# Two reorderings in a fused transposed-attention and binary-convolution kernel: where the first term of a depthwise convolution is issued, and in what pieces the last units are stored

## The chip, the cores and the metric

The kernel runs on one core of one Trainium2 chip. The metric is the device time of one execution in microseconds (us), as the median of several executions. The profile is one further execution, taken by the hardware profiler; its span (from the first to the last instruction) is about 2 us shorter than the device time. Engines are named as the profile names them: PE is the matrix engine and PEld its weight loads, DVE the vector engine, ACT the scalar engine, POOL the GpSimd engine, SP the engine that here only issues transfers. `ACTq` and `SPq` are the instruction queues of ACT and SP, from which transfers are issued. A label such as L382 is a line of the kernel.

## The reference, cut to what matters

The input is one image of 384 channels and 192 x 192 pixels. Layer 0 normalises it by groups, makes q, k and v by a 1x1 convolution, takes the maximum over 2x2 pixels, applies a 3x3 depthwise convolution, lets the channels of a head attend to each other, and projects. Layer 1 is a 1x1 convolution with binary weights on signs of shifted channels. Both add their input.

```python
qkv = jnp.einsum('bchw,oc->bohw', x, w_qkv) + b_qkv[None, :, None, None]
qkv = qkv.reshape(b, 3 * c, hs, DS, ws, DS).max(axis=(3, 5))
qkv = lax.conv_general_dilated(qkv, w_dw, (1, 1), 'SAME', feature_group_count=3 * c, ...)
qkv = qkv + b_dw[None, :, None, None]
q, k, v = jnp.split(qkv, 3, axis=1)
# ... cut: q and k normalised, attn = q k^T over pixels, four top-k softmaxes
out = _topk_softmax(attn, C // 2) @ v * a1 + ...      # three more of the same form
out = jax.nn.gelu(out, approximate=False)
out = repeat each pixel 2 x 2; out = jnp.einsum('bchw,oc->bohw', out, w_proj) + b_proj
# layer 0: x = x + L0(group_norm(x))
# layer 1: x = x + einsum(shifted sign(group_norm(x)), sign(weight)) + bias
```

## The kernel before

The image is cut into 24 units of 8 rows (4 rows after the maximum). The kernel makes four passes: sums for the normalisation; q and k (with the products q k^T); v with the attention applied to it; and a last pass with projection, residual, binary convolution and the store. Within a pass each unit has three tiles of 128 channels, m = 0, 1, 2.

In the v pass the result of the convolution goes to a `chunk`, which holds the rows of four units (UC = 4, CR = 16 rows of 96 columns). The convolution of unit u makes the rows 4u - 1 to 4u + 2, because its last row needs the next unit. So for u = 4, 8, 12, 16 and 20 one of the four rows belongs to the chunk before and three to the next: such a tile crosses a chunk, and `parts` has two entries, of 96 and of 288 elements per partition, instead of one of 384.

```python
# v pass
lo, hi = rows(u)
first = PR * u - 2 + lo
last = first + hi - lo
for m in range(CT):
    parts = []
    for c in range(first // CR, last // CR + 1):
        r0, r1 = max(first, c * CR), min(last, c * CR + CR - 1)
        parts.append(
            (chunk[c][:, m, (r0 - c * CR) * WP : (r1 + 1 - c * CR) * WP], r0 - first, r1 + 1 - r0)
        )
    if qkv_unit(pqkv, xt, u, 2 * CT + m, pool[m], parts, amid=lambda: block and next(block, 1)):
        block = None
    # ... cut
```

One tile is made in `qkv_unit`. Three blocks of 512 pixels are multiplied on PE (nine products, 18 instructions in the trace), each into one of three PSUM buffers; DVE takes the maximum out of each (L364) and so frees it. ACT adds the bias to the four new rows (L373). Then comes the convolution, nine terms on each part: the first on ACT (L380), eight on DVE (L382), each of which needs the one before. The first row of a part needs `pl` rows 0, 1 and 2; rows 0 and 1 are the last two of the unit before, copied there by ACT (L385), and only row 2 is new. `amid` lets a block of the attention be issued (`ops` in the trace: 32 matrix instructions into four PSUM buffers, emptied by ACT with GELU, L671).

```python
for r0, nr, c0, ncol in BLOCKS:
    ps = pqkv.tile([P, 512], F32, name="qkv")          # three buffers
    for t in range(CT):
        ins = nc.tensor.matmul(ps, wq[:, t, m * P : (m + 1) * P], x4[...], ...)   # L354
        # ... cut
    nc.vector.tensor_reduce(pl[...], ps.rearrange(...), AX.XY, ALU.max)           # L364
# ... cut
new = pl[:, 2 : 2 + PR, 1 : 1 + WP]
nc.scalar.activation(new, new, AF.Identity, bias=bq[:, m : m + 1])                # L373
for acc, r0, n in parts:
    acc2 = acc.rearrange("p (r w) -> p r w", w=WP)
    for k in range(9):
        r = lo - 1 + r0 + k // 3
        src = pl[:, r : r + n, k % 3 : k % 3 + WP]
        if k == 0:
            nc.scalar.activation(acc2, src, AF.Identity, bias=..., scale=...)     # L380
        else:
            nc.vector.scalar_tensor_tensor(acc2, src, wdw[:, m, k : k + 1], acc2, ALU.mult, ALU.add)  # L382
result = amid()
if u < NU - 1:
    nc.scalar.copy(pl[:, 0:2, :], pl[:, PR : PR + 2, :])                          # L385
```

In this pass the order of each engine's instructions is not that of the program: the compiler sets it beforehand, from the dependences and from its own estimate of when each instruction can start. On the chip the order is then fixed. `tc.keep_in_program_order(ins)` pins `ins` behind the instruction that the program has just before it on the same engine.

The last pass is issued in the order of the program. Its units go through `finished(i, m)`: two groups of four rows, each with six matrix products (L844) and one DVE addition (L856) into `xt`. The last three units, i = 21, 22, 23, are stored from there.

```python
def finished(i, m):
    u = order[i]
    xt, sg = kept[u], signs[i % NSIGN]
    for r0 in range(0, UR, 4):
        # ... cut: matmuls of four rows into ps (L844)
        last = (i, m) == (NU - 1, CT - 1)
        for js in (range(1), range(1, 2)) if last else (range(2),):
            px = slice((r0 + 2 * js[0]) * W, (r0 + 2 * js[-1] + 2) * W)
            blk = xt[:, m, px].rearrange("p (j n) -> p j n", j=len(js))
            nc.vector.scalar_tensor_tensor(blk, ps[...], bl1[:, m : m + 1], blk, ALU.add, ALU.add)   # L856
            if last:
                (nc.scalar if js[0] else nc.sync).dma_start(ov[u, :, m, px], xt[:, m, px])           # L860
    if i + 3 >= NU and (i, m) != (NU - 1, CT - 1):
        nc.sync.dma_start(ov[u, :, m], xt[:, m])                                                     # L862
```

Of the kernel before, what the change touches and what calls it, by code (L numbers as in the profile page):

```python
# [15 lines left out]
AF = mybir.ActivationFunctionType  # L16
# [6 lines left out]
CT = C // P  # L23
# [9 lines left out]
NU = H // UR  # L33
# [116 lines left out]
def conv_preact_kernel(ctx: ExitStack, tc: tile.TileContext, a: dict, out: bass.AP):  # L150
    nc = tc.nc
    xv = a["x"].rearrange("u t p n -> u p t n")
    ov = out.rearrange("u t p n -> u p t n")
# [10 lines left out]
    parts = {name: small[:, i:j] for name, i, j in SMALL}  # L164
    ind = parts["ind"].rearrange("p (t g) -> p t g", t=CT)
    bpr, bl1, bq, bdw, temp = (parts[i] for i in ("b_proj", "bias", "b_qkv", "b_dw", "temp"))
    wdw = parts["w_dw"].rearrange("p (m k) -> p m k", m=NM)
# [11 lines left out]
    def unit(u, pool=big, parts=1, pieces=1):  # L179
        xt = pool.tile([P, CT, UPX], F32, name="xt", tag="big")  # L180
        n = CT // parts
        for t in range(0, CT, n):

            for j in range(0, UPX, UPX // pieces if t == CT - 1 else UPX):
                px = slice(j, j + UPX // pieces if t == CT - 1 else UPX)
                nc.sync.dma_start(xt[:, t : t + n, px], xv[u][:, t : t + n, px])  # L186
        return xt
# [71 lines left out]
    with tc.tile_pool(name="p1", bufs=1, side="right") as p1, tc.tile_pool(name="p1ps", bufs=2, space=PSUM) as psp:  # L259
# [17 lines left out]
        for i in range(NU):  # L277
            u = NU - 1 - i
            xt = unit(u, parts=CT if u in (0, 1, NU - 1) else 1, pieces=1 if u else UPX // 512)
# [62 lines left out]
    def rows(u):  # L342

        return (1 if u else 2), (PR if u < NU - 1 else PR + 1)

    def qkv_unit(pqkv, xt, u, m, pl, parts, before=None, amid=lambda: None):


        x4 = xt.rearrange("p t (r w) -> p t r w", w=W)
        lo, hi = rows(u)  # L350
        for r0, nr, c0, ncol in BLOCKS:
            ps = pqkv.tile([P, 512], F32, name="qkv")
            for t in range(CT):
                ins = nc.tensor.matmul(  # L354
                    ps,
                    wq[:, t, m * P : (m + 1) * P],
                    x4[:, t, r0 : r0 + nr, c0 : c0 + ncol],
                    start=(t == 0),
                    stop=(t == CT - 1),
                )  # L360
                if m == CT and t == r0 == c0 == 0:

                    tc.keep_in_program_order(ins)
            nc.vector.tensor_reduce(  # L364
                pl[:, 2 + r0 // 2 : 2 + (r0 + nr) // 2, 1 + c0 // 2 : 1 + (c0 + ncol) // 2],
                ps.rearrange("p (i a j b) -> p i j a b", a=2, b=2, j=ncol // 2),
                AX.XY,
                ALU.max,
            )
        if before:  # L370
            before()
# [5 lines that stand above are left out]
                r = lo - 1 + r0 + k // 3  # L377
                src = pl[:, r : r + n, k % 3 : k % 3 + WP]
                if k == 0:
                    nc.scalar.activation(acc2, src, AF.Identity, bias=bdw[:, m : m + 1], scale=wdw[:, m, 0:1])  # L380
                else:
                    nc.vector.scalar_tensor_tensor(acc2, src, wdw[:, m, k : k + 1], acc2, ALU.mult, ALU.add)  # L382
        result = amid()
        if u < NU - 1:
            nc.scalar.copy(pl[:, 0:2, :], pl[:, PR : PR + 2, :])  # L385
        return result
# [4 lines left out]
    with pairs, tc.tile_pool(name="p2t", bufs=2, side="right") as tp:  # L391
# [61 lines left out]
        for u in range(NU):  # L453

            for v in range(u, u + KEEP + 1):
                if v not in kept:
                    kept[v] = unit(v % NU)
            xt = kept.pop(u)
            lo, hi = rows(u)
            n = hi - lo + 1  # L460
            for m in range(2 * CT):
                acc = tp.tile([P, (PR + 1) * WP], F32, name="dw")[:, : n * WP]
                qkv_unit(pqkv, xt, u, m, padded_qk[m], [(acc, 0, n)], None if u or m else lambda: bias(gram[0][:, :NM]))
                transposed(u, *divmod(m, CT), acc)
                sq = tp.tile([P, (PR + 1) * WP], BF16, name="sq", bufs=1)
                nc.scalar.activation(sq[:, : n * WP], acc, AF.Square, accum_out=ssq[:, m, u : u + 1])  # L466

                if m == CT - 1 and u and (u % 2 == 0 or u == NU - 1):
                    for v in range(max(u - 2, 0) if u % 2 == 0 else u - 1, u):
                        products(v)  # L470
                if m % CT == CT - 1:
                    moved(u, m // CT)
# [141 lines left out]
    with ExitStack() as vs:  # L614
# [67 lines left out]
        for u in range(NU):  # L682
            xt = kept.pop(NU + u) if NU + u in kept else unit(u)
# [7 lines left out]
# [3 lines that stand above are left out]
# [5 lines left out]
                if qkv_unit(pqkv, xt, u, 2 * CT + m, pool[m], parts, amid=lambda: block and next(block, 1)):  # L699
                    block = None  # L700
# [61 lines left out]
    with end:  # L762
# [9 lines left out]
        def rows_of(ts, p, at=0, pitch=PITCH, n=W):  # L772
            return ts[p, at : at + UR * pitch].rearrange("p (r w) -> p r w", w=pitch)[:, :, :n]
# [62 lines left out]
# [5 lines that stand above are left out]
                ps = psp.tile([P, 2, 512], F32, name="l1ps")  # L841
                for j in range(2):
                    for t in range(CT):
                        nc.tensor.matmul(  # L844
                            ps[:, j, : 2 * W],
                            wb[:, t, m * P : (m + 1) * P],
                            rows_of(sg, slice(0, P), SAT[t])[:, r0 + 2 * j : r0 + 2 * j + 2],
                            start=(t == 0),
                            stop=(t == CT - 1),
# [6 lines that stand above are left out]
                    nc.vector.scalar_tensor_tensor(  # L856
                        blk, ps[:, js[0] : js[-1] + 1, : 2 * W], bl1[:, m : m + 1], blk, ALU.add, ALU.add
                    )
                    if last:
                        (nc.scalar if js[0] else nc.sync).dma_start(ov[u, :, m, px], xt[:, m, px])  # L860
            if i + 3 >= NU and (i, m) != (NU - 1, CT - 1):
                nc.sync.dma_start(ov[u, :, m], xt[:, m])  # L862

        def stored(i):

# [12 lines left out]
        with tc.manual_schedule():  # L878
            v = todo.pop(0)
            kept[v] = unit(v, more, parts=CT)  # L880
            for i in range(4):
                for m in range(CT):
                    summed(i, m)
                if i < 2:
                    signed(i)

            for i in range(NU):
                ahead = range(1, 5), range(6, NU - 2)
                for m in range(CT):
                    for r, k in zip(ahead, (3, 2)):  # L890
                        if i in r:
                            summed(i + k, m)
                    finished(i, m)
                if i + 2 < NU:
                    signed(i + 2)
# [72 lines left out]
```

## Time and profile before

| what | value |
|---|---|
| device time, median of 3 | 2214.27 us (2213.98 to 2215.72) |
| span of the profiled execution | 2211.8 us |
| granted PE clock, mean | 0.999 |
| first convolution term into chunk (L380) | 87 instructions, 15 of them of 96 elements |
| DVE terms into chunk (L382) | 696 instructions |
| last PE matmul of v's 1x1 convolution | about 1900 us |
| last DVE addition (L856) ends | about 2205.7 us |

The page of the profile gives busy times by engine, then the span in 40 slices, the queues, the chain of work that ended last, and the costliest groups. A group's row reads: line, engine, operation, output<-inputs, shapes, count, then busy time and mean duration, then idle time of that engine before these instructions and what ended it. In a timeline each row has its start, the time that it covers, the engine, the line, and in brackets the idle time before it and what released it; a row may hold several instructions of one line.

### The profile page before, as it was taken

How to read it: one execution, taken by the hardware profiler on the slowest of the kernel's cores; microseconds unless marked ns; L12 is line 12 of the kernel's file. 1: busy time of each engine (PE TensorE's matmuls, PEld its weight loads, DVE VectorE, ACT ScalarE, POOL GpSimd, SP SyncE). 2: the span in 40 equal slices, each digit the busy share in tenths (PEclk: the TensorE clock that was granted, in tenths of full speed). 3: DMA queues.
4: the chain of work that ended last, by engine and by line, in shares of the span. 5: the costliest groups of instructions: out<-in, count | busy, mean ns of one | idle time of the engine just before them, and what ended most of it. 6: DMA issues, size and time to landing. Idle time of an engine off the chain costs nothing.

```text
span 2211.8 us, 20840 instructions
## 1 busy us (share of the span) xinstructions
PE 2055.5 (93%) x6701; PEld 960.5 (43%) x6701; DVE 1906.0 (86%) x3272; ACT 909.1 (41%) x1637; POOL 211.2 (10%) x330
## 2 busy tenths in 40 slices
PE   0049999999999999999999999999999999999998
PEld 0024444444444444444444444444444444455555
DVE  5677988989898898988889899988878787899998
ACT  4542222222222222222222221225556556598785
POOL 1000000000000000000000000000000000087775
PEclk9999999999999999999999999999999999999999
DMA  9972222222222232222223212113222212379997
GB/s 398 418 287 64 65 67 73 85 87 72 68 64 69 72 98 74 74 66 66 69 70 107 67 32 102 54 71 155 86 86 78 94 43 86 129 309 406 425 424 317
DMA packets 210013, 302.75 MB, mean 137 GB/s; under 512 B 162256, under 2 KB 165616, under 8 KB 209904
## 3 DMA queue, kind: packets, MB, share of 16 engines
q1 hardware_dynamic: 199296, 247.78, 32.1%
q10 hardware_dynamic: 10608, 53.64, 5.9%
q8 instruction: 53, 0.87, 0.2%
q14 instruction: 56, 0.46, 0.1%
HBM read 216.04 MB, written 56.62 MB: 123 GB/s over the span
## 4 chain that ended last, share of the span: by engine, by line
PE 75%; DVE 13%; DMA 5%; ACT 4%; SPq 1%; issue 1%; POOL 0%; DVEq 0%; ACTq 0%
PE qkv L354 60%; DVE chunk L382 7%; PE l1ps L844 6%; PE yps L593 5%; DMA xt<-in_x_dram 5%; DVE pooled L364 3%; ACT chunk L671 2%; PE gram L443 2%; DVE dw L382 1%; PE ops L648 1%; ACT chunk L380 1%; SPq L186 1%; ACT pooled L373 1%; DVE xt L605 1%; PE qkv L273 0%
## 5 line engine op out<-in xcount | busy, mean ns | idle before, releaser
L354 PE MATMUL qkv<-xt,wq 128*128 128x512 f32 x3888 | 1678.6, 593 | 3.7 <-DVE pooled L364 3.7
L354 PEld LDWEIGHTS qkv<-xt,wq 128*128 128x128 f32 x3888 | 735.5, 190 | 932.8 <-issue 827.8
L382 DVE SCALAR_TENSOR_TENSOR dw<-pooled,small,dw 128x384 f32<-128x384 f32 (+2 forms) x1152 | 708.3, 615 | 86.1 <-ACT dw L380 60.8
L364 DVE TENSOR_REDUCE pooled<-qkv 128x128 f32<-128x512 f32 x648 | 441.3, 683 | 64.4 <-PE qkv L354 64.1
L382 DVE SCALAR_TENSOR_TENSOR chunk<-pooled,small,chunk 128x384 f32<-128x384 f32 (+3 forms) x696 | 371.7, 546 | 78.0 <-ACT chunk L380 60.2
L385 ACT COPY pooled<-pooled 128x196 f32<-128x196 f32 x207 | 73.6, 356 | 664.0 <-DVE dw L382 543.6
L373 ACT ACTIVATE pooled<-pooled,small 128x384 f32<-128x384 f32 x216 | 133.0, 616 | 421.9 <-DVE pooled L364 408.6
L825 ACT ACTIVATE signs<-xt,nmean 64x1536 fp8e4<-64x1536 f32 x144 | 226.5, 1573 | 39.5 <-PE yps L593 25.6
L844 PE MATMUL l1ps<-signs,wb 128*128 128x384 fp8e4 x864 | 152.3, 326 | 0.2
L856 DVE SCALAR_TENSOR_TENSOR xt<-l1ps,small,xt 128x768 f32<-128x768 f32 (+1 forms) x146 | 138.6, 997 | 0.0
L273 PE MATMUL qkv<-wq,late 128*32 128x384 f32 x18 | 8.1, 609 | 140.4 <-ACT late L295 140.4
L593 PE MATMUL yps<-chunk,wpr 128*128 128x384 f32 x384 | 134.2, 486 | 0.3 <-DVE xt L605 0.3
L671 ACT ACTIVATE chunk<-ops 32x512 f32<-32x512 f32 (+3 forms) x220 | 129.7, 589 | 8.7 <-PE ops L648 4.4
L605 DVE SCALAR_TENSOR_TENSOR xt<-yps,small,xt 128x768 f32<-128x768 f32 x128 | 124.2, 1012 | 9.2 <-PE yps L593 2.1
L301 DVE BATCH_NORM_STATS2 room<-xt 128x6 f32<-128x512 f32 x144 | 88.1, 678 | 51.1 <-DMA xt<-in_x_dram 51.0
L622 POOL MEMSET pooled<- 128x196 f32 x3 | 0.8, 263 | 1281.8 <-DVE dw L382 1281.8
L844 PEld LDWEIGHTS <-wb 128*128 128x128 fp8e4 x864 | 83.6, 97 | 72.7 <-issue 14.3
L466 ACT ACTIVATE sq<-dw 128x384 bf16<-128x384 f32 (+2 forms) x144 | 75.3, 523 | 76.3 <-DVE dw L382 76.3
L380 ACT ACTIVATE dw<-pooled,small 128x384 f32<-128x384 f32 (+2 forms) x144 | 100.1, 695 | 1.5
L290 ACT ACTIVATE room<-xt 128x1536 bf16<-128x1536 f32 x48 | 71.2, 1483 | 66.5 <-DMA xt<-in_x_dram 65.7
L593 PEld LDWEIGHTS yps<-chunk,wpr 128*128 128x128 f32 x384 | 71.3, 190 | 39.6 <-PE yps L593 0.9
L412 DVE STREAM_TRANSPOSE blocks<-dw 128x384 f32<-128x384 f32 (+1 forms) x144 | 82.3, 572 | 4.6
(119 smaller groups left out, 596.9 us busy)
## 6 DMA issues: line engine op xcount, KB each, us to landing
xt<-in_x_dram SPq DMA_DIRECT2D x81, 2304.0 KB, 14.7
out_dram<-xt ACTq DMA_DIRECT2D x17, 2304.0 KB, 15.6
room<-blocks SPq DMA_DIRECT2D x736, 36.0 KB, 2.0
xt<-in_x_dram SPq DMA_DIRECT2D x26, 768.0 KB, 8.4
out_dram<-xt ACTq DMA_DIRECT2D x12, 768.0 KB, 8.7
out_dram<-xt SPq DMA_DIRECT2D x8, 768.0 KB, 5.2
wq<-in_w_qkvT_dram ACTq DMA_DIRECT2D x1, 1728.0 KB, 15.0
room<-blocks SPq DMA_DIRECT2D x32, 48.0 KB, 2.0
```

The costliest lines, as they stand in the source:

```text
L301: nc.vector.bn_stats(stats[b][:, t, at : at + 6], xt[:, t, j * 512 : (j + 1) * 512])
L354: ins = nc.tensor.matmul(ps, wq[:, t, m * P : (m + 1) * P], x4[:, t, r0 : r0 + nr, c0 : c0 + ncol], start=(t == 0), stop=(t == CT - 1),)
L364: nc.vector.tensor_reduce(pl[:, 2 + r0 // 2 : 2 + (r0 + nr) // 2, 1 + c0 // 2 : 1 + (c0 + ncol) // 2], ps.rearrange("p (i a j b) -> p i j ...
L373: nc.scalar.activation(new, new, AF.Identity, bias=bq[:, m : m + 1])
L380: nc.scalar.activation(acc2, src, AF.Identity, bias=bdw[:, m : m + 1], scale=wdw[:, m, 0:1])
L382: nc.vector.scalar_tensor_tensor(acc2, src, wdw[:, m, k : k + 1], acc2, ALU.mult, ALU.add)
L593: nc.tensor.matmul(ps, wpr[:, t, m * P : (m + 1) * P], o[:, t, :], start=(t == 0), stop=(t == CT - 1),)
L605: nc.vector.scalar_tensor_tensor(x5[:, m, r], yb, bpr[:, m : m + 1], x5[:, m, r], ALU.add, ALU.add)
L671: ins = nc.scalar.activation(chunk[c][to : to + k, t, cols], ps[at + j : at + j + k], AF.Gelu, accum_out=osum[to : to + k, t, g : g + 1],)
L825: nc.scalar.activation(rows_of(sg, p, SAT[t] - HSHIFT[t][h]), xt[p, t, :].rearrange("p (r w) -> p r w", w=W), AF.Sign, bias=nmean1[p, t : ...
L844: nc.tensor.matmul(ps[:, j, : 2 * W], wb[:, t, m * P : (m + 1) * P], rows_of(sg, slice(0, P), SAT[t])[:, r0 + 2 * j : r0 + 2 * j + 2], sta ...
L856: nc.vector.scalar_tensor_tensor(blk, ps[:, js[0] : js[-1] + 1, : 2 * W], bl1[:, m : m + 1], blk, ALU.add, ALU.add)
```

## The change

The first part pins the first term of a part that belongs to a crossing tile behind the instruction that ACT has before it in the program. For the first part that is the bias of the tile, for the second part the first term of the first part. What it is for: the first term of the one-row part reads only a row that is there since the unit before, so the compiler is free to issue it early; the pin takes that freedom away.

The second part stores the tiles of the last three units, except the very last tile, in two transfers of four rows (384 KB) instead of one of eight rows (768 KB): each is issued as soon as its own addition is done. The very last tile keeps its four transfers of 192 KB.

```diff
@@ -377,7 +377,10 @@
                 src = pl[:, r : r + n, k % 3 : k % 3 + WP]
                 if k == 0:
-                    nc.scalar.activation(acc2, src, AF.Identity, bias=bdw[:, m : m + 1], scale=wdw[:, m, 0:1])
+                    ins = nc.scalar.activation(acc2, src, AF.Identity, bias=bdw[:, m : m + 1], scale=wdw[:, m, 0:1])
+                    if len(parts) > 1:
+
+                        tc.keep_in_program_order(ins)
                 else:
                     nc.vector.scalar_tensor_tensor(acc2, src, wdw[:, m, k : k + 1], acc2, ALU.mult, ALU.add)
@@ -856,10 +859,11 @@
                         blk, ps[:, js[0] : js[-1] + 1, : 2 * W], bl1[:, m : m + 1], blk, ALU.add, ALU.add
                     )
+
+                    if i + 3 >= NU and not last:
+                        nc.sync.dma_start(ov[u, :, m, px], xt[:, m, px])
                     if last:
                         (nc.scalar if js[0] else nc.sync).dma_start(ov[u, :, m, px], xt[:, m, px])
-            if i + 3 >= NU and (i, m) != (NU - 1, CT - 1):
-                nc.sync.dma_start(ov[u, :, m], xt[:, m])
```

## The prediction

> **What bounds the kernel now.** I read the page first, for the whole, then the chain of work that ended last, PE's waits in the v pass, the timelines of PE, ACT and DVE around one crossing, and short windows at the end. Times are us from the start of the span.
>
> ```profile
> PE 2055.5 (93%) x6701; PEld 960.5 (43%) x6701; DVE 1906.0 (86%) x3272; ACT 909.1 (41%) x1637; POOL 211.2 (10%) x330
> PE 75%; DVE 13%; DMA 5%; ACT 4%; SPq 1%; issue 1%; POOL 0%; DVEq 0%; ACTq 0%
> ```
>
> PE is the bound, DVE close behind it. Neither part of the change touches work of PE, so it can only win gaps of PE, or the drain at the end. The gaps of PE in the v pass, from its waits between 1480 and 1900:
>
> ```profile
> PE qkv L354 <- DVE pooled L364: 3.7, 4, 1.0
> PE ops L648 <- ACT chunk L671: 2.6, 3, 0.9
> ```
>
> So 6.3 us in all, in seven gaps. The timeline of PE shows where they lie (the crossing of unit 16; those of 12 and 20 look the same, 104.3 us earlier and later):
>
> ```profile
> 1674.42 23.44 PE L354 MATMUL qkv<-xt,wq 128*128 128x512 f32 x54
> 1697.79 1.97 PE L648 MATMUL ops<-chunk,aT 32*64 32x512 f32 x32
> 1699.69 7.99 PE L354 MATMUL qkv<-xt,wq 128*128 128x512 f32 x18
> 1708.68 15.72 PE L354 MATMUL qkv<-xt,wq 128*128 128x512 f32 x36 [0.99 <-DVE pooled L364]
> 1724.33 1.08 PE L648 MATMUL ops<-chunk,aT 32*64 32x512 f32 x6
> 1726.27 1.96 PE L648 MATMUL ops<-chunk,aT 32*64 32x512 f32 x26 [0.86 <-ACT chunk L671]
> ```
>
> The row at 1697.79 is a normal attention block: 32 matmuls in 1.9 us. The one after the crossing takes 1724.33 to 1728.23, 3.9 us, because ACT still held PSUM buffers. So a crossing costs 0.99 + 2.0 = 3.0 us. Unit 8 (0.71 of wait, and 2.6 instead of 1.9 for the block) loses about 1.4, and unit 4 nothing: sum 3 x 3.0 + 1.4 = 10.4 us. That is the most that the first part can bring.
>
> Why PE waits there, from DVE and ACT:
>
> ```profile
> 1698.56 0.85 DVE L382 SCALAR_TENSOR_TENSOR chunk<-pooled,small,chunk 128x96 f32<-128x96 f32 x2 [0.35 <-ACT chunk L380]
> 1699.33 0.68 DVE L364 TENSOR_REDUCE pooled<-qkv 128x128 f32<-128x512 f32 x1
> 1699.93 8.10 DVE L382 SCALAR_TENSOR_TENSOR chunk<-pooled,small,chunk 128x96 f32<-128x96 f32 x17
> 1707.94 1.88 DVE L364 TENSOR_REDUCE pooled<-qkv 128x128 f32<-128x512 f32 x3
> ...
> 1705.14 0.47 ACT L380 ACTIVATE chunk<-pooled,small 128x96 f32<-128x96 f32 x1
> ```
>
> ACT runs 96-element first terms in unit 15, before unit 16 has a bias. They release five of the eight DVE terms that need old rows only. The row at 1699.93 holds 17 terms, eight of 384 and nine of 96 elements, without a maximum (L364) between; PE needs a free buffer at 1707.5, and the first is freed about 0.6 after 1707.94. Unit 15 would have needed eight. The late maximum makes the next bias late, then the GELUs behind it in ACT's order, then PE's attention block.
>
> **What the Trainium skill says.** "PSUM — Partial Sum Buffer", section "Engine vs sequencer instructions": the queues of ACT and DVE are strictly first in, first out. The trace agrees: three finished maxima start only at 1707.94, after all 17 terms. "Perfetto Trace Analysis", "Identifying Performance Opportunities": a gap that repeats on the saturated engine can mean that there is too little PSUM for the next tile. It does repeat, at 1.0 and 0.9 us, but the buffers suffice in the units between. "Perfetto Trace Analysis", "DMA Optimizations": splitting transfers lets some start sooner where the DMA engines have idle time, and larger ones use the bandwidth better. Both apply at the end; below.
>
> **First part, step by step.** Nothing is added or removed but order: 15 first terms of 96 elements, with 75 early DVE terms behind them, move from the unit before a crossing into the crossing unit.
>
> Gain in unit 15: without the two terms at 1698.56 its DVE stays on the pattern of unit 14, where the maximum at 1672.85 was followed by eight terms at 1674.96 and two maxima at 1680.07, 7.55 us after the attention block began at 1672.52. Here that gives 1697.79 + 7.55 = 1705.3, and the buffer is free at 1705.9, before 1707.5. So the 0.99 goes. The third maximum moves from about 1709.2 to 1707.5, ACT gains about 2 us, and most of the 2.0 us of the attention block goes too; a rest of 0.3 I keep, since three instructions of 0.62 + 0.47 + 0.63 now stand ahead of the GELUs where there were 0.62 + 0.71. Gain 2.7 of 3.0.
>
> Cost in unit 16: by form, DVE terms of 96, 288 and 384 elements take 314, 514 and 615 ns, but start every 0.33, 0.53 and 0.65. A crossing tile now has 8 x 0.33 + 8 x 0.53 = 6.9 us of terms in one piece, a wait for ACT of 0.62 + 0.49 = 1.1, and 3 x 0.6 of maxima: 9.8 us if nothing fills the wait, 8.7 if all does. PE needs 7.8 for such a tile, and 25.3 for three with an attention block. So DVE falls behind by 26.1 - 25.3 = 0.8 to 29.4 - 25.3 = 4.1 us in a crossing unit. It had less to do there before, and waited for PE:
>
> ```profile
> 1727.86 5.16 DVE L382 SCALAR_TENSOR_TENSOR chunk<-pooled,small,chunk 128x96 f32<-128x96 f32 x11 [0.68 <-ACT pooled L373]
> 1732.94 1.36 DVE L364 TENSOR_REDUCE pooled<-qkv 128x128 f32<-128x512 f32 x2
> 1736.18 0.69 DVE L364 TENSOR_REDUCE pooled<-qkv 128x128 f32<-128x512 f32 x1 [1.88 <-PE qkv L354]
> ```
>
> The x11 are one tile's late terms, three of 96 and eight of 288, again in one piece. With the pin these would be 16, and last 5 x 0.3 = 1.6 us longer, and start 0.5 later. PE comes to this point some 2.8 us earlier than before, DVE about 1 us earlier. Before, buffers were free 1736.0 - 1733.5 = 2.5 us ahead of need; now 2.5 - 1.6 - 0.5 - 1.8 = -1.4. Maxima that slip between the last terms can take half of this away. I put 0.4 to 1.4, say 0.9, here, and 0.4 at the tile after it, where DVE is still behind. The three units that follow have slack (1.10 of DVE waiting for PE in one tile), so it doesn't carry to the next crossing.
>
> Balance: 2.7 - 1.3 = 1.4 us at each of 12, 16 and 20; about 0.5 at 8; about -0.5 at 4, where DVE was busy without a break (30.00 of 30.00 us from 1395 to 1425, with the softmax in its free slots). Sum 4.2 + 0.5 - 0.5 = 4.2 us. The last crossing is 75 us before the pass ends, and the last pass runs on PE, so what is won before then reaches the end.
>
> **Second part.** The end, by stretches (after the busy times come the clock, the DMA share and GB/s):
>
> ```profile
> 2193.00:2194.00 1.00, 0.99 (x7) 0.49 (x6) 1.00 (x2) 1.00 (x1) 0.94 (x2) 1.00 0.21 80
> 2194.00:2195.00 1.00, 1.00 (x8) 0.60 (x7) 1.00 (x2) 0.97 (x2) 0.78 (x3) 1.00 0.00 0
> 2196.00:2204.00 8.00, 8.00 (x51) 4.71 (x49) 8.00 (x10) 0.00 (x0) 1.94 (x2) 1.00 1.01 409
> 2206.00:2208.00 2.00, 0.00 (x0) 0.00 (x0) 0.00 (x0) 0.00 (x0) 0.00 (x0) 1.00 0.98 368
> ```
>
> From about 2195.1 the DMA engines are full until the end, seven tiles of 786 kB at 409 GB/s, 13.4 us. Ahead of that they are idle for 1.9 us, for want of a finished tile. With halves the first of these seven can go one addition earlier: 0.97 us. From then on PE makes a tile in 1.97 us, 399 GB/s, so the engines stay nearly full. Against it: rows of 3 KB instead of 6 KB. The last quarters (1.5 KB rows) moved at 368 against 409; a fixed cost per row drawn through these two gives 395 at 3 KB, an estimate, so 13.4 us become 13.9. Net gain 0.97 - 0.5, about 0.4 us. Eight more issues of 0.33 us on SP have 0.97 us each and cost nothing.
>
> **Sum.** 4.2 + 0.4 = 4.6 us: 2214.3 - 4.6 = 2209.7, rounded 2210.
>
> **The rivals.** *The load only moves.* DVE has the same total across a crossing, so the stall of unit 15 may come back whole in unit 16 or 17 (16 terms in one piece, where 17 stalled PE). For it: the sum of -1.4 above, and the x11 in one piece. Against: before, DVE still had 1.88 + 0.25 us of waiting for PE in that unit. It would give 2213 to 2217. *The pin wins nearly all,* since the maxima fit between the terms: up to 10 us, 2204. For it: the row of eight at 1719.63 was followed by maxima with two and four terms between. Against: two chains of terms fill each other's gaps, and then no maximum gets in. *A new order everywhere behind unit 4,* because the compiler sets the order by its own estimate: a few us either way, which I can't read from the profile. *The stores matter more or less:* between +0.5, if small rows cost more, and -0.9.
>
> **Range and chances.** The uncertain terms are four crossings at 1.4 +- 1.5 us, which go together, unit 4 at +-1, and the end at +-0.5: about +-5 us. I take 2204.5 to 2216. Both 2% bounds (44 us) are out of reach of gaps of 10 us, and no step can lose 44 us: within 2% 0.98. Some gain is likelier than some loss, about three to one.
>
> **What would show it.** Right: no L380 of 96 elements ahead of the bias of its own tile; the 17 terms at unit 15 become eight, and PE's gaps of 0.99 before the crossing and 0.86 at the attention block are gone, while new gaps of 0.5 to 1.5 stand one or two tiles later; DMA without the 1.9 us hole near the end, and GB/s somewhat under 409. Wrong: PE waits over 6.3 us in the v pass, or under 1; a PE gap near unit 4 of over 1 us; a change of total that the v pass and the end don't hold.

## The result, and the profile after

| | before | after |
|---|---|---|
| device time, median | 2214.12 us | 2204.18 us (2204.04 to 2204.77) |
| ratio, 95% interval | | 0.9954 (0.9937 to 0.9972) |
| span of the profiled execution | 2211.8 us | 2202.4 us |
| v pass on PE: from the first long row of the 1x1 convolution after the last `p3ps` of the softmax (1357.46 before, 1357.75 after) to the row behind the last attention block inside the pass (1883.00, 1874.63) | 525.54 us | 516.88 us |
| drain: from the end of the last addition to the end of the span | 6.07 us | 4.99 us |

The kernel is 9.9 us faster, and 2210 (2204.5 to 2216) was predicted. Of the 9.4 us of span, 8.7 lie in the v pass and 1.1 in the drain; 0.3 went the other way ahead of the v pass, where its start varies from run to run by up to 1.7 us. That is why the experiments below are compared by the length of the v pass. PE's last matmul of v's 1x1 convolution ends at 1914.2 us before (not at about 1900, as the table above has it) and at 1905.8 after.

The page of the kernel after, first its busy times and then the shares of the chain that ended last:

```profile
PE 2052.6 (93%) x6701; PEld 961.6 (44%) x6701; DVE 1900.2 (86%) x3272; ACT 906.5 (41%) x1637; POOL 212.0 (10%) x330
PE 84%; DVE 8%; DMA 6%; SPq 1%; ACT 1%; issue 0%; POOL 0%; ACTq 0%; DVEq 0%
```

The counts are the same, as they must be: only order changed. In the chain, PE has taken 9 points, mostly from DVE and ACT: the path now runs along PE through the crossings. PE's waits between 1340 and 1900:

```profile
PE qkv L354 <- DVE pooled L364: 0.9, 1, 0.9
PE p3ps L506 <- DVE dg L504: 0.3, 1, 0.3
```

Seven gaps of 6.3 us have become one of 0.9; the other line, of the softmax, is in both kernels. The same crossing as in the prediction, that of unit 16, in the timeline of PE after:

```profile
1695.13 1.97 PE L651 MATMUL ops<-chunk,aT 32*64 32x512 f32 x32
1697.03 23.44 PE L354 MATMUL qkv<-xt,wq 128*128 128x512 f32 x54
1720.40 2.25 PE L651 MATMUL ops<-chunk,aT 32*64 32x512 f32 x32
```

The 54 matmuls are not broken, and the attention block takes 2.25 us instead of 3.9. From crossing to crossing (rows of 54 at 1621.15 and 1722.58) it is 101.43 us where it was 104.28. The timeline of DVE in the crossing unit after:

```profile
1714.96 5.06 DVE L385 SCALAR_TENSOR_TENSOR chunk<-pooled,small,chunk 128x96 f32<-128x96 f32 x15 [1.04 <-ACT chunk L380]
1719.93 0.69 DVE L364 TENSOR_REDUCE pooled<-qkv 128x128 f32<-128x512 f32 x1
1720.53 0.52 DVE L385 SCALAR_TENSOR_TENSOR chunk<-pooled,small,chunk 128x288 f32<-128x288 f32 x1
1720.96 1.29 DVE L364 TENSOR_REDUCE pooled<-qkv 128x128 f32<-128x512 f32 x2
1723.29 5.61 DVE L385 SCALAR_TENSOR_TENSOR chunk<-pooled,small,chunk 128x96 f32<-128x96 f32 x16 [1.04 <-ACT chunk L380]
1728.81 1.28 DVE L364 TENSOR_REDUCE pooled<-qkv 128x128 f32<-128x512 f32 x2
1730.61 0.69 DVE L364 TENSOR_REDUCE pooled<-qkv 128x128 f32<-128x512 f32 x1 [0.52 <-PE qkv L354]
```

And that of ACT, at the first of the three tiles:

```profile
1713.95 0.62 ACT L373 ACTIVATE pooled<-pooled,small 128x384 f32<-128x384 f32 x1 [1.04 <-DVE pooled L364]
1714.47 0.97 ACT L380 ACTIVATE chunk<-pooled,small 128x96 f32<-128x96 f32 x2
```

ACT now has the two first terms directly behind the bias. The row that matters is x16: all terms of a crossing tile in one piece, eight of 96 and eight of 288 elements, in 5.61 us. The x11 of before, five terms fewer, took 5.16. Between the first term and the last the two parts alternate in DVE's order: 96, 288, 96, 288.

At the end, in stretches of the kernel after (columns as in the prediction; the last two are the DMA share and GB/s):

```profile
2184.00:2185.00 1.00, 1.00 (x7) 0.55 (x6) 1.00 (x3) 0.97 (x2) 0.94 (x2) 1.00 0.86 335
2185.00:2186.00 1.00, 0.99 (x7) 0.54 (x6) 1.00 (x3) 0.99 (x1) 0.85 (x2) 1.00 0.08 31
2186.00:2194.00 8.00, 8.00 (x51) 4.71 (x50) 8.00 (x9) 1.57 (x1) 2.99 (x4) 1.00 0.98 379
2194.00:2198.00 4.00, 2.11 (x13) 1.04 (x11) 3.41 (x6) 0.00 (x0) 0.00 (x0) 1.00 1.02 397
```

The hole in the transfers is about 1.1 us long (0.14 and 0.92 idle), where it was 1.9. Then they run under the 409 GB/s of before.

### The profile page after: what moved, and what is told of

Read it like the earlier page. It is cut to its first block, busy times and chain, and to the rows that moved or that the text cites. A ratio compares the mean times of both kernels' runs of the same rounds, so it can differ in the third digit from the quotient of the medians.

```text
span 2202.4 us, 20861 instructions
## 1 busy us (share of the span) xinstructions
PE 2052.6 (93%) x6701; PEld 961.6 (44%) x6701; DVE 1900.2 (86%) x3272; ACT 906.5 (41%) x1637; POOL 212.0 (10%) x330
## 4 chain that ended last, share of the span: by engine, by line
PE 84%; DVE 8%; DMA 6%; SPq 1%; ACT 1%; issue 0%; POOL 0%; ACTq 0%; DVEq 0%
PE qkv L354 69%; PE l1ps L847 6%; PE yps L596 5%; DMA xt<-in_x_dram 5%; DVE chunk L385 3%; PE gram L446 2%; DVE pooled L364 2%; DVE dw L385 1%; PE ops L651 1%; DVE xt L608 1%; DMA wq<-in_w_qkvT_dram 1%; SPq L186 0%; PE qkv L273 0%; SPq L433 0%; ACT chunk L380 0%
## 5 line engine op out<-in xcount | busy, mean ns | idle before, releaser
L385 DVE SCALAR_TENSOR_TENSOR chunk<-pooled,small,chunk 128x384 f32<-128x384 f32 (+3 forms) x696 | 363.6, 546 | 77.5 <-ACT chunk L380 68.1
```

## The experiments

All times are medians; "before" was 2214.4 beside the runs e1 to e7 (with the repeat of the changed kernel) and 2213.8 beside e8, e9 and e4b. Line numbers differ by a few between kernels.

**Each part alone.** e1 has the pin and the old stores, e2 the new stores and no pin:

```diff
 # e1: stores as before
-                    if i + 3 >= NU and not last:
-                        nc.sync.dma_start(ov[u, :, m, px], xt[:, m, px])
+            if i + 3 >= NU and (i, m) != (NU - 1, CT - 1):
+                nc.sync.dma_start(ov[u, :, m], xt[:, m])
 # e2: no pin
-                    if len(parts) > 1:
+                    if False:
```

> The pin without the new stores. Theory A (the pin frees PE in the v pass, the stores only shorten the drain): the v pass ends as early as in the changed kernel, PE's last matmul of the 1x1 convolution at about 1905.8 us, and the drain from the last addition to the end of the span is that of before, 6.1 us: time 2205.2 us, 1.0 to 1.1 above the changed kernel. Rival B (part of the 8.3 us by which the last pass starts earlier comes from elsewhere, run to run): over 2206.5 us.

> The stores in halves without the pin. Theory A: the two parts add up, v pass as before with 6.3 us of PE waits, drain 5.0 instead of 6.1 us: 2213.1 us, 1.0 below before. The prediction's sum for the stores gave 0.4 us, 2213.8. Rival B (the halves gain only because the last pass starts at another time): no change, 2214.2.

| | time | ratio to before | v pass | drain |
|---|---|---|---|---|
| e1, pin only | 2206.01 | 0.9962 (0.9950 to 0.9975) | 516.82 | 6.08 |
| e2, stores only | 2213.41 | 0.9997 (0.9988 to 1.0005) | 525.58 | 5.38 |
| both, once more (a2) | 2204.45 | 0.9958 (0.9945 to 0.9970) | 516.80 | 5.43 |

> The changed kernel once more, as the measure for the runs beside it: 2204.2 us, drain 5.0 us.

The parts are independent: the v pass follows the pin alone to within 0.1 us. The pin is worth 8.4 us of time. e1's time is 0.8 above theory A's, but its v pass and its drain are those of theory A. The stores are worth 1.0 by e2, but that interval contains no change, and 1.6 by e1 against a2; the drains of the profiles in these tables differ by 0.6 to 1.1. So about 1 us, with its first digit uncertain.

**Why the crossing unit bears its load.** e3 keeps all of the change, but in a crossing tile the terms of the second part are issued behind those of the first. Same instructions, same sizes; DVE only loses the alternation:

```diff
-                    nc.vector.scalar_tensor_tensor(acc2, src, wdw[:, m, k : k + 1], acc2, ALU.mult, ALU.add)
+                    ins = nc.vector.scalar_tensor_tensor(acc2, src, wdw[:, m, k : k + 1], acc2, ALU.mult, ALU.add)
+                    if len(parts) > 1 and r0 > 0 and k == 1:
+                        tc.keep_in_program_order(ins)
```

> The changed kernel, but in a crossing tile the terms of the 288-element part are issued behind all terms of the 96-element part, so that DVE no longer alternates between two independent chains. Theory C (alternating terms start sooner one after the other, 16 terms in 5.6 us, and this is why the crossing unit bears its load): a tile's 16 terms take about 6.7 to 6.9 us of DVE without the maxima, DVE falls behind by 3 to 4 us in a crossing unit, and PE waits again, 1 to 1.5 us at each of four or five crossings: 2208 to 2211 us. Rival D (it is the place of the early terms alone that matters, and the crossing unit had the slack anyway; maxima slip between the terms of one chain): 2204 to 2205.5 us with hardly a wait of PE.

Measured 2207.68 us, ratio 0.9971 (0.9960 to 0.9982), v pass 520.06: 3.2 us longer than with alternation. PE's waits in e3, then DVE at the crossing of unit 16:

```profile
PE qkv L354 <- DVE pooled L364: 3.9, 5, 0.8
```

```profile
1722.56 0.68 DVE L364 TENSOR_REDUCE pooled<-qkv 128x128 f32<-128x512 f32 x1
1723.16 8.63 DVE L385 SCALAR_TENSOR_TENSOR chunk<-pooled,small,chunk 128x288 f32<-128x288 f32 x19
1731.71 1.88 DVE L364 TENSOR_REDUCE pooled<-qkv 128x128 f32<-128x512 f32 x3
```

Here 19 terms stand in one piece (by form eight of 96 and eleven of 288), and 8 x 0.33 + 11 x 0.53 = 8.5 us, at the prediction's starts for single chains, against 8.63 read. The same stretch from the second tile's first term on:

```profile
1724.69 7.10 DVE L385 SCALAR_TENSOR_TENSOR chunk<-pooled,small,chunk 128x96 f32<-128x96 f32 x16
```

So from the first of the tile's 16 terms to the maximum behind them it is 1731.71 - 1724.69 = 7.0 us, and 1728.81 - 1723.29 = 5.5 in the kernel after. PE waits 0.7 to 0.8 at each of the five crossings. Theory C holds in kind: without alternation a wait of 0.8 on a maximum is back, where 1.0 stood before the change, now one unit later. The 2.0 us that the attention block lost before the change are not back. The wait is smaller than C gave (0.8, not 1 to 1.5), and the time is just under C's range; maxima do slip between the terms of one chain in the tile before (rival D's point), though not enough.

**Unit 4.** e4, run twice (e4b), pins at units 8, 12, 16 and 20 only:

```diff
-                    if len(parts) > 1:
+                    if len(parts) > 1 and u > UC:
```

> The changed kernel with the pin for units 8, 12, 16 and 20 only, not for 4. Theory A: the one remaining wait of PE on a maximum (0.85 us at 1421, unit 4) and 0.4 us around it are gone, since unit 4 had no wait before: 2202.9 us, 1.3 below the changed kernel. Rival (the order behind unit 4 changes as a whole and the wait comes back at unit 8): 2204 to 2205.

> The changed kernel with the pin on ACT for units 8, 12, 16 and 20 only, once more, as the measure for the two beside it: 2203.5 us.

Measured 2203.61 and 2203.31 us, ratios 0.9954 (0.9942 to 0.9967) and 0.9952 (0.9939 to 0.9964), v pass 515.70 and 515.64: 1.2 shorter, with no wait of PE on a maximum left. So at unit 4 the pin costs 1.2 us. There, in the kernel after, the first crossing tile's terms run in one piece from 1415.71 to 1420.76, while PE needs a buffer at 1420.57.

**What stalled PE: the early instruction on ACT, or the early terms on DVE?** e5 frees ACT's first term again and pins DVE's first term of the first part instead:

```diff
-                    if len(parts) > 1:
-                        tc.keep_in_program_order(ins)                # ACT, k == 0
+                    if len(parts) > 1 and r0 == 0 and k == 1:
+                        tc.keep_in_program_order(ins)                # DVE, k == 1
```

> The pin moved from ACT to DVE: the 96-element first term on ACT is free again and comes early, as before the change, but the first DVE term of that part is held behind the maxima of its own tile. Theory A (what stalled PE were the early DVE terms in the unit before, 17 in one piece, not the early instruction on ACT): PE's waits stay away in units 8 to 20, and since ACT has one instruction less between the bias and the GELUs, the attention block of a crossing takes 1.9 to 2.0 us instead of 2.25: 2203 us, 1 to 1.5 below the changed kernel. Rival (the early ACT instruction itself holds up ACT and PE): waits of 0.9 come back, 2207 us or more.

The timeline of ACT in e5, then those of DVE and of PE:

```profile
1701.77 0.47 ACT L380 ACTIVATE chunk<-pooled,small 128x96 f32<-128x96 f32 x1
1706.26 0.61 ACT L373 ACTIVATE pooled<-pooled,small 128x384 f32<-128x384 f32 x1 [4.03 <-DVE pooled L364]
```

```profile
1698.05 5.20 DVE L382 SCALAR_TENSOR_TENSOR chunk<-pooled,small,chunk 128x384 f32<-128x384 f32 x8 [0.90 <-ACT chunk L380]
1703.17 1.28 DVE L364 TENSOR_REDUCE pooled<-qkv 128x128 f32<-128x512 f32 x2
```

```profile
1720.88 2.02 PE L650 MATMUL ops<-chunk,aT 32*64 32x512 f32 x32
```

ACT's 96-element term comes in unit 15, ahead of unit 16's bias, as before the change; DVE's piece is eight terms and not 17; PE has one wait of 0.7 (unit 4) and none at the other crossings. So the early terms on DVE were the cause, and ACT's instruction only what let them loose. The time was 2204.13 us, ratio 0.9956 (0.9942 to 0.9969), not the 2203 expected: the attention block fell to 2.02 us as foreseen, but that is 0.23 at each of three crossings, and the v pass was only 0.7 shorter (516.22).

**Which halves shorten the drain.** e6 stores in halves in the first of the last three units only (i = 21), e7 in the last two only:

```diff
-                    if i + 3 >= NU and not last:
+                    if i == NU - 3 and not last:          # e6;  e7: i >= NU - 2
                         nc.sync.dma_start(ov[u, :, m, px], xt[:, m, px])
# and whole tiles, as before, for the other of the three units
```

> The changed kernel with stores in halves for the first of the last three units only, whole tiles for the other two. Theory of the prediction (a half fills the idle stretch of the DMA engines before the saturated end, and small rows cost something in the saturated end): drain 4.6 us, 2203.7. Rival F (the gain is at the end: with halves less is queued ahead of the last quarters): drain near 6 us, 2205.

> The changed kernel with stores in halves for the last two units only, whole tiles for the first of the last three. Theory of the prediction: the idle stretch stays 1.9 us long, small rows cost 0.4: drain 6.1 to 6.5 us, 2205.5. Rival F: drain 5.0 us, 2204.2.

e6: 2204.76 us, ratio 0.9957 (0.9944 to 0.9969), drain 5.89. e7: 2205.32 us, 0.9961 (0.9949 to 0.9974), drain 6.27. In e7 the hole stays, as the prediction's view had it (three stretches, 1 us each, from 1 us after the row of last additions begins):

```profile
2186.28:2187.28 1.00, 0.99 (x7) 0.58 (x6) 1.00 (x3) 0.97 (x2) 0.84 (x2) 1.00 0.00 0
2187.28:2188.28 1.00, 1.00 (x8) 0.58 (x6) 1.00 (x2) 1.00 (x1) 0.94 (x2) 1.00 0.26 106
2188.28:2189.28 1.00, 1.00 (x8) 0.58 (x6) 1.00 (x2) 0.53 (x1) 0.47 (x2) 1.00 1.04 430
```

In e6 that hole is shortened, but a new one opens 2 us later, where the first whole tile is waited for:

```profile
2185.76:2186.76 1.00, 1.00 (x8) 0.58 (x6) 1.00 (x2) 1.00 (x1) 0.94 (x2) 1.00 1.04 401
2186.76:2187.76 1.00, 1.00 (x8) 0.58 (x6) 1.00 (x2) 0.53 (x1) 0.47 (x2) 1.00 0.84 323
2187.76:2188.76 1.00, 1.00 (x8) 0.58 (x6) 1.00 (x2) 0.00 (x0) 0.94 (x2) 1.00 0.48 197
2188.76:2189.76 1.00, 1.00 (x9) 0.59 (x7) 1.00 (x2) 0.00 (x0) 0.63 (x1) 1.00 1.00 412
```

The expectation of 4.6 us for e6 took a start won early as kept. But a half in hand (0.39 MB) is moved in about 1 us, while a whole tile takes two additions, 1.85 us, so the engines run empty again where the pieces become whole, for 0.16 + 0.52 = 0.7 us. Rival F's numbers for e6 (near 6 us, 2205) are about those read, but in e7 it is the prediction's view whose numbers came (6.1 to 6.5 us, 2205.5) and not F's (5.0, 2204.2). That only halves in all three units keep the lead is not shown: e6's time lies within the range of the changed kernel's (2204.1 to 2205.9 in a2).

**The gains together, and a second queue.** e8 joins e5 and e4 (DVE's term pinned, `u > UC`, stores in halves). e9 also issues second halves of the last two units from ACT:

```diff
 # e8, on e5
-                    if len(parts) > 1 and r0 == 0 and k == 1:
+                    if len(parts) > 1 and u > UC and r0 == 0 and k == 1:
 # e9, on e8
-                        nc.sync.dma_start(ov[u, :, m, px], xt[:, m, px])
+                        (nc.scalar if r0 and i > NU - 3 else nc.sync).dma_start(ov[u, :, m, px], xt[:, m, px])
```

> The pin on DVE's first term instead of ACT's, and for units 8, 12, 16 and 20 only, with the stores in halves. If the two gains seen apart add up (the v pass was 1.2 us shorter without the pin at unit 4 and 0.6 shorter with the pin on DVE), the v pass is 1.5 us shorter than in the changed kernel and the time 2202.8 us; if the DVE pin gained only at unit 4, it equals the run without the pin at unit 4, 2203.5.

> The same, but in the last two units the second half of a tile is issued from ACT instead of SP. If the drain is set by when additions end and by what the DMA engines move (the view so far), it stays at 5.0 to 5.4 us: no change, 2202.8. If the issue on SP holds stores back at the end (issues of up to 1.1 us were seen there), the drain shortens to 4.5: 2202.2.

e8: 2202.59 us (2202.34 to 2203.73), ratio 0.9949 (0.9935 to 0.9962), v pass 514.98, 1.9 shorter than in the changed kernel. e9: 2202.78 us, ratio 0.9949 (0.9937 to 0.9961), v pass 514.98, drain 5.45. The two gains in the v pass add up. The second queue brings nothing to be seen: the 0.6 us expected if issue on SP held the stores back did not come. The drain with halves everywhere lies between 4.99 and 6.21 us in the profiles; the two longest (6.05 in e8, 6.21 in e4b) were read in executions at the upper end of their kernels' times, as was e7's 6.27, so a drain from one profile is good to half a microsecond at best. Over the nine profiles with halves everywhere it is 5.5 on average, against 6.1 with whole tiles. By its median e8 is the fastest kernel here: 11.2 us under the "before" beside it, where the changed kernel had 9.9. The intervals of the two ratios overlap; the shorter v pass, 514.98 in both e8 and e9, does not depend on that.

## Why the prediction was right or wrong

**The bound and the ceiling: right.** Only gaps of PE and the drain could be won, 10.4 us in the v pass at most. The v pass gave 8.7, and no other stage moved.

**"Gain 2.7 of 3.0" at a crossing: right.** The gap of 0.99 is gone. The attention block takes 2.25 us, so that 0.35 is left of the loss, where the prediction kept "a rest of 0.3". The pattern of unit 14 did come back: terms at 1697.58 and maxima at 1702.69, 7.56 us behind the attention block at 1695.13, where 7.55 was used. e5 shows the cause as stated: the early DVE terms in one piece ahead of the maxima.

**"8 x 0.33 + 8 x 0.53 = 6.9 us of terms in one piece": this term failed.** It measures 5.61. The starts of 0.33 and 0.53 us were read where DVE works on one chain, in which each term needs the one before. For that order the price was right: e3, with one chain behind the other, took 7.0 us for the tile. But in a crossing tile the pin lets DVE alternate between two chains, and a pair takes 5.61 / 8 = 0.70 us on average instead of 0.86. That is 1.3 us for a tile and 3.9 for a crossing unit, nearly the whole upper end of the lag that I worked out (4.1). I had seen that two chains "fill each other's gaps", and used it only against the maxima, not for the length.

**"2.5 - 1.6 - 0.5 - 1.8 = -1.4", and the cost of 1.3 taken from it: wrong by that term.** Instead of 1.6 the five more terms cost 5.61 - 5.16 = 0.45. The start was 0.37 later (0.5 allowed). DVE lost 0.63 against PE up to there (its maximum moved from 1726.50 to 1721.56, PE's restart from 1728.15 to 1722.58), not 1.8, since the crossing tile before, with x15 in 5.06 us, was short as well. 2.5 - 0.45 - 0.37 - 0.63 = 1.05 us to spare, and the trace has it: a buffer free at 1729.4, needed at 1722.58 + 7.8 = 1730.4. No gap at all. With 0 in place of 1.3 the prediction's balance at units 12, 16 and 20 would have been 3 x 2.7 = 8.1 us; read are 3 x 2.85 = 8.55. Unit 8 gave 1.2 (0.5 predicted), and with unit 4 that is 8.55 + 1.2 - 1.1 = 8.65, against 8.66 read. e3 is the counter-test: without alternation PE waits 0.8 at each of these crossings, near the 0.9 that the prediction put there. Its further 0.4 "at the tile after it" came in neither kernel. From crossing to crossing e3 takes 102.22 us (attention blocks at 1619.48 and 1721.70), so that 2.06 of the 2.85 are gained without alternation, where 1.4 was predicted, and 0.79 by it. Of the signs that the prediction named, the old gaps went and the new ones of 0.5 to 1.5 stayed away except at unit 4; 0.9 us of waits in all is under the 1 that it named as a sign of being wrong.

**Unit 4: right sign, -1.12 instead of -0.5.** DVE was busy there without a break, as the prediction said, and the moved terms now stand ahead of the maximum that PE waits for, 0.85 us at 1421.42; without the pin at unit 4 that wait is gone (e4).

**The stores: right in kind, too small.** 0.4 was predicted; the times give about 1, the average of the drains 0.6. The hole became 0.8 us shorter (0.97 predicted), and the transfers after it ran near the 395 GB/s estimated (379 to 397, against 409 for whole tiles). One reading was wrong, "PE makes a tile in 1.97 us, 399 GB/s". That is PE's own pace, but DVE comes behind it and adds without a break:

```profile
2184.06 13.35 DVE L859 SCALAR_TENSOR_TENSOR xt<-l1ps,small,xt 128x768 f32<-128x768 f32 x16
```

The first twelve of these sixteen additions make four rows each and start 0.925 us apart, so a tile becomes ready in 1.85 us, at 425 GB/s, more than the engines move. The prediction's two terms, with the values read, would still give only about 0.4; where the rest comes from stays open, since drains of the same stores differ by more than that.

**The range.** The rival "the pin wins nearly all" is what happened, but not, as put there, because the maxima fit between the terms: the tile's 16 terms stayed in one piece, which alternation made short enough. The range ended 0.3 us above the result since the crossings, which go together, all carried the mis-sized cost of 1.3.

## What to carry to other kernels

A start-to-start time read in one chain of dependent instructions isn't the cost of an instruction: where two independent chains are at hand, price the alternating order before calling an engine overloaded. Work moved from one stretch to another may change its own length by that. Where a transfer can start earlier because the first piece is small, see whether the engines run empty again when the next piece is large (0.7 us in e6).

## What the runs showed of the hardware that was not expected

The recorded durations of DVE's terms on 384 and 96 elements give a slope of (615 - 314) / 288 = 1.045 ns per element; the Trainium skill, "Vector Engine (DVE) Microarchitecture Reference", section "Measured stream behaviour on trn2", states 1.0417 for the built-in operations that it measured, and about 75 ns per instruction besides. Here more comes besides, and it depends on the order. Inside one chain the terms start every 0.354, 0.554 and 0.654 us (96 and 288 elements in e3, 384 in the kernel before), which leaves 0.25 us each beside 0.10, 0.30 and 0.40. While two chains alternate, the starts in the kernel after are 0.229 us apart behind a term of 96 and 0.429 behind one of 288 (1724.96, 1725.19, 1725.62), which leaves 0.13. The additions of the last pass, none of which needs the one before, show the same: 0.925 us apart on 768 elements, 0.80 + 0.12.

The recorded durations hardly differ: 0.314 us for a term of 96 while chains alternate, 0.319 in one chain. In one chain the next term starts 0.035 us after the recorded end of the one before; in alternation it starts 0.085 us before it. That the difference is the wait for the result before fits the dependences; the runs show the difference, not its inner cause. Only the start-to-start time tells the two cases apart.
